# Moving gate steps between the halves of a head, loading W_qr by whole rows, and fetching the second group's tokens earlier in a four-block transformer kernel

## The chip, the cores and the metric

The kernel runs on one core of one Trainium2 chip. The metric is the device time of one execution in microseconds (us); the time of a version is the median of its runs. The engines are named as in the profile: PE is TensorE's matmul, PEld its weight load, DVE is VectorE, ACT is ScalarE, POOL is GpSimd, and SP is SyncE, which issues most plain DMAs here. POOL issues the indirect ones (gathers and scatters by row numbers).

## The reference

Everything is fp32; there are 16 sequences of 256 tokens, 512 wide, so 4096 tokens. Four blocks follow each other, each with a residual, the first three on a layer norm:

```python
x = x + conv_mix(layernorm(x), k, bias, ctx, ctx, 8)         # block 1
x = x + routed_and_shared_ffn(layernorm(x), gate_w, ...)     # block 2
x = x + latent_attention(layernorm(x), ctx, itok, W_...)     # block 3
x = x + gelu(x @ proj1.T + b1) @ proj2.T + b2                # block 4
```

- Block 1: within each channel group, all 8 x 8 products of heads of `v` and `x2` are convolved causally along the width of 512 with a filter per group (in the reference by FFT), `bias` times the product is added, and the result is summed with `x1`.
- Block 2: `logits = x @ gate_w` over 8 experts; the two largest are taken, their softmax are the gates. The result is the sum over the two chosen experts of gate times `gelu(x @ w1 + b1) @ w2 + b2` (hidden width 256), plus a shared FFN of width 512.
- Block 3: keys and values come from the context through a latent of 128, queries through a latent of 192; 16 heads of 128, and a rotary part of 64 in query and key (`W_qr`, `W_kr`). A query with segment number s sees the keys s-8 to s. The output goes through `W_o`.
- Block 4: a dense FFN of width 2048 with gelu.

## The kernel before

The work goes in tiles of 128 tokens and in stages, one after another on PE.

**Convolution, gates and shared FFN** (`conv_shared`, until about 980 us). One tile is a "head" h, 0 to 31. The causal convolution is done as matmuls with Toeplitz blocks: `conv` (L292) makes `y` from `kv` and `ut`, where `kv` holds the products of heads. Each head goes through `conv` in two halves of four column blocks `lc`. After each block, DVE multiplies and reduces `y` (`pr` L297, `oT` L304) and makes one block of the next half's `kv` (L274). Between the halves PE transposes the next head's inputs: `turn_inputs` makes `pvt` (L258), which needs the buffer that the last `kv` has read. The order of PE, DVE and ACT is the order of the program text here (`manual_schedule`); POOL and SP are placed by a scheduler by priorities. Small pieces of other work are given to `conv` as lists by `lc`: `one` for the first half, `two` for the second; lists `mid` and `end` are run between and after the halves.

The gates belong to groups of four heads, one group behind. With q = h % 4: q = 0 makes the logits, q = 1 runs `tops` in three steps, q = 2 makes row numbers (`slots`) and gate shares, and from q = 2 on rows of tokens are scattered to the experts (`send`, POOL L371). The steps of `tops`: step one finds the first maximum, step two the second, step three (L437 to L445) makes `ex` (difference, then an exponential on ACT), `both` (sum of the two one-hot rows) and four running counts `came`. In the kernel before all three stand in the first half, at `lc` 0, 1 and 2. `rank_rows`, at the end of the head, reads `both` and `came` on PE. The last tiles' gates are made in one piece each at the end of the stage.

**Routed experts** (`routed`, about 980 to 1300 us). 71 tiles of gathered rows (`xg`, four buffers), for each the two expert layers (L895, L914). Beside it, `beside` prepares the attention in steps numbered by the tile i: `head_weights` folds weight matrices through four rotating buffers `pre` (also to be had as `spare`), tile 12 loads the latent weights and `W_qr` (`load_latents(apart=True)`), tile 16 the routes (`load_routes`, which begins with an iota on POOL and works out `slot_s`, the rows of expert results of each sorted token), and from tile 20 on one step of the list `early` is run per tile: four `fetch` and three `fetch_keys`.

**Attention** (`attention_sorted`, about 1300 to 2243 us). Tokens are sorted by segment; T = 0 to 31 are tiles of sorted tokens, four to a group. For a tile, `fetch` gathers token rows and rotary rows (POOL L1902), `fetch_routed` the two rows of expert results, through four shared buffers `g_yt`, `fetch_keys` four windows of keys. `tokens` adds the expert results times their gates to the rows (DVE L1440), normalizes (`xh`, L72 and the statistics before it) and transposes on PE (`pt` L99; the rotary rows `prr` L1448). `latents` makes a group's `q1` and `q0` (`pq`, L1459), `heads` the queries of all heads (PE `pqr`, `pqn` L1487 to L1498), turned by the rotary angles on ACT, DVE and POOL (L1503 to L1507). Then per tile: `scores` (L1555), `weigh` (DVE transpose L1565, mask L1567, maximum), `weights` (exponential on ACT L1576, sum, division, transpose), `window` of the next tile (keys, ACT `kn` L1523, mask on DVE), `values`, and two tiles later `project` (`po`, L1611). Group 0 has its heads in two halves: after T = 0 and after T = 1, half of the pairs for the tiles 2 and 3. The second group's fetches (T = 4 to 7) come after T = 1 and T = 2 in the program, and its tokens after T = 2 and at T = 3. `issue_after(x)` keeps what is in it behind the instruction x in the scheduler's order. Outside `conv_shared` each engine's order is the scheduler's.

**Last FFN** (from about 2243 us): matmuls L1804 and L1862. No line of it is touched.

Of the kernel before, what the change touches and what calls it, by code (L numbers as in the profile page):

```python
# [42 lines left out]
class Kernel:  # L43
# [59 lines left out]
    def conv_shared(self, x1d, xgd):  # L103
        nc, tc, a = self.nc, self.tc, self.a
        with ExitStack() as ctx:
# [304 lines left out]
            def tops(r):  # L410
# [25 lines left out]
                def three():  # L436
                    r["ex"] = ex = g2("ex")  # L437
                    nc.vector.tensor_tensor(ex, r["m2"], r["m1"], ALU.subtract)
                    nc.scalar.activation(ex, ex, AF.Exp)
                    r["both"] = both = rp.tile([P, T4, E], F32, tag="both", name="both")[:, 0:n, :]  # L440
                    nc.vector.tensor_tensor(both, r["oh1"], r["oh2"], ALU.add)
                    for t in range(r["h"], r["h"] + n):
                        nc.vector.tensor_tensor(
                            came[:, t + 1, :], came[:, t, :], both[:, t - r["h"], :], ALU.add
                        )  # L445
# [297 lines left out]
            with tc.manual_schedule(engines=order):  # L743
                for h in range(HC):
# [19 lines left out]
                    if before is not None:  # L764
# [6 lines left out]
                        elif q == 1:  # L771
                            steps = tops(st["r"])
                            one = {k: [steps[k]] for k in range(3)}
# [185 lines left out]
    def load_latents(self, apart=False):  # L959
# [6 lines left out]
        if apart:  # L966
            f = R // 2
            for d in range(2):
                for c in range(2):
                    lo, to = (2 * d + c) * f, (2 * c + d) * f  # L970
                    nc.sync.dma_start(
                        self.wqr0.rearrange("q (h m) -> q h m", m=P)[:, :, to : to + f],
                        a["W_qr"][0:P, :].rearrange("q (h m) -> q h m", m=P)[:, :, lo : lo + f],
                    )
                    for i in range(2):
                        nc.sync.dma_start(
                            self.wqr1[i * (QC - P) : (i + 1) * (QC - P), :, to : to + f],
                            a["W_qr"][P:QC, :].rearrange("q (c i m) -> q c i m", i=2, m=P)[:, :, i, lo : lo + f],
                        )
            return  # L980
        nc.sync.dma_start(self.wqr0, a["W_qr"][0:P, :])
        for i in range(2):
# [3 lines left out]
            )  # L986

    def load_routes(self, tmp):
# [7 lines left out]
        nc.gpsimd.iota(  # L996
            start, pattern=[[ROOM, E]], base=0, channel_multiplier=0, allow_small_or_imprecise_dtypes=True
        )
# [62 lines left out]
    def beside(self, i, half, heads, early):  # L1061
# [4 lines left out]
        if half == 0:  # L1066
            heads(min(max(i - 2, 0), 2 * HEADS - 6))
            if i == 12:
                self.load_latents(apart=True)
            if i == 16:  # L1070
                self.load_routes(self.spare())
            if 20 <= i < 20 + len(early):
                early[i - 20]()
# [278 lines left out]
    def fetches(self, pool, x1d):  # L1352
# [7 lines left out]
        def fetch(T):  # L1360
            xs[T] = xt = tp.tile([P, D], F32, tag="xt", name="xt", bufs=XT_BUFS)
            self.fetch_rows(xt, x1f, self.order[:, T : T + 1], TOK)
            rrs[T] = rr = tp.tile([P, 2, P], F32, tag="rr", name="rr", bufs=4)
# [7 lines left out]
        return fetch, fetch_keys, xs, rrs, gws  # L1371

    def attention_sorted(self, fetched, ygd, x3s, end_of_queries):
        nc, tc = self.nc, self.tc
        wdq, m0, m1, wqr0, wqr1, nw = self.wdq, self.m0, self.m1, self.wqr0, self.wqr1, self.nw
        fetch, fetch_keys, xs, rrs, gws = fetched
# [5 lines left out]
        with ExitStack() as ctx:  # L1382
# [257 lines left out]
            for T in range(NT_ + 2):  # L1640
                g, t = T // T4, T % T4
                if T < NT_:
# [6 lines left out]
                    if nxt is not None:  # L1649
                        for k in () if g == 0 else ((0,), (2,), (), ())[t]:  # L1650
                            fetch((g + 1) * T4 + k)
                            fetch_routed(nxt, k)
                    if nxt is not None and g == 0 and t == 3:
# [6 lines left out]
                if T < NT_:  # L1660
# [3 lines left out]
                    if T < 2:  # L1664
                        for two in range(T * HP // 4, (T + 1) * HP // 4):
                            turned = heads(state[0], two, parts[1])
                    if nxt is not None and t == 3:
# [16 lines left out]
                if T < NT_ and nxt is not None:  # L1684
                    if g == 0:
                        if t == 1:
                            with tc.issue_after(turned):
                                for k in range(TH):
                                    fetch(T4 + k)
                                    fetch_routed(nxt, k)  # L1690
                        if t == 2:
                            for k in range(TH):
                                tokens(nxt, k)
                                fetch(T4 + TH + k)
                                fetch_routed(nxt, TH + k)
# [211 lines left out]
    def run(self, out):  # L1907
# [34 lines left out]
        with ExitStack() as experts:  # L1942
# [4 lines left out]
            with ExitStack() as stack:  # L1947
# [3 lines left out]
                early += [lambda t=t: fetched[1](t) for t in range(3)]  # L1951
                self.routed(xgd, ygd, early)
# [116 lines left out]
```

## Time and profile before

| what | value |
|---|---|
| median of 3 runs | 3085.8 us (3085.61 to 3088.05) |
| profiled execution, its own time | 3089.02 us |
| its span | 3087.2 us |
| PE busy | 3006.9 us (97%) |
| DVE busy | 1440.7 us (47%) |
| POOL busy | 912.5 us (30%) |
| ACT busy | 658.0 us (21%) |
| mean granted clock of PE | 0.99 of full speed |
| PE idle in wait of `kv` (L274) | 24.1 us, 11 times |
| PE idle in wait of `xh` (L72) | 24.4 us, 10 times |

A row of the timeline has start and duration in us, engine, line, operation, output and inputs, shape, how many instructions are drawn together (x4), and in brackets the idle time of the engine before it with what ended it. In a table by windows each row is a stretch of time: its length, the busy time of each engine with the number of instructions, the granted PE clock, the DMA engines' share and GB/s. Busy time that overlaps in other engines costs nothing; the span is set by what ends last, here PE almost throughout.

### The profile page before, as it was taken

What the parts mean: (1) busy time and instruction counts of PE and PEld (TensorE: products, weight loads), DVE (VectorE), ACT (ScalarE), POOL (GpSimd) and SP (SyncE); (2) the same over time, 40 slices, a digit from 0 to 9 for tenths busy, and PEclk for the clock granted to TensorE, in tenths of its full rate; (3) what the DMA queues carried; (4) which work ended last, traced back from release to release, by engine and by line L of the source; (5) the groups of instructions that cost most, each with busy time, mean ns of one, the idle gap of its engine ahead of it and who ended that gap; (6) DMA issues with size and microseconds to landing.
All of it is one profiled execution on the core that took longest, in us unless ns stands there. A gap on an engine that the chain in (4) does not pass through costs nothing.

```text
span 3087.2 us, 34716 instructions
## 1 busy us (share of the span) xinstructions
PE 3006.9 (97%) x12825; PEld 1530.4 (50%) x12825; DVE 1440.7 (47%) x2684; ACT 658.0 (21%) x1248; POOL 912.5 (30%) x1232
## 2 busy tenths in 40 slices
PE   8999999999999999898999999999999999999998
PEld 4444444544445666563554554554444444444443
DVE  6777777677674444443433433433433232222222
ACT  1111111111111121153333333323111111111110
POOL 2233332232234000066545545544110300301201
PEclk9999999999999999998999999999999999999999
DMA  4222211211216643312211211211221100100100
GB/s 118 69 99 85 69 57 53 75 53 55 65 44 192 183 155 128 110 53 64 90 49 49 82 56 50 74 49 58 73 102 28 55 14 14 55 11 8 47 1 29
DMA packets 124722, 209.87 MB, mean 68 GB/s; under 512 B 33864, under 2 KB 53736, under 8 KB 123904
## 3 DMA queue, kind: packets, MB, share of 16 engines
q1 hardware_dynamic: 96256, 125.63, 13.7%
q0 software_dynamic: 28288, 81.92, 8.3%
q8 instruction: 105, 1.72, 0.2%
q14 instruction: 73, 0.60, 0.1%
HBM read 140.12 MB, written 67.37 MB: 67 GB/s over the span
## 4 chain that ended last, share of the span: by engine, by line
PE 84%; DVE 6%; issue 5%; POOL 3%; DMA 1%; ACT 0%; SPq 0%; POOLq 0%; DVEq 0%; ACTq 0%
PE y L292 15%; PE po L1862 14%; PE ph L1804 12%; PE po L1611 8%; PE phg L895 4%; PE pog L914 4%; PE pout L503 4%; PE pqn L1490 4%; PE ph L490 3%; PE pqr L1487 2%; PE pqn L1498 2%; PE pt L99 2%; DVE oT L304 1%; PE pqr L1494 1%; DVE pr L297 1%
## 5 line engine op out<-in xcount | busy, mean ns | idle before, releaser
L292 PE MATMUL y<-kv,ut 128*128 128x512 f32 x1280 | 566.4, 598 | 0.6 <-DVE pr L297 0.6
L1611 PE MATMUL po<-nw,w 128*128 128x512 f32 x1024 | 445.7, 593 | 0.0
L1862 PE MATMUL po<-p,ht 128*128 128x512 f32 x1024 | 445.1, 592 | 0.0
L292 PEld LDWEIGHTS y<-kv,ut 128*128 128x128 f32 x1280 | 243.8, 193 | 298.8 <-issue 288.6
L1611 PEld LDWEIGHTS po<-nw,w 128*128 128x128 f32 x1024 | 192.0, 190 | 235.1 <-issue 229.6
L1862 PEld LDWEIGHTS po<-p,ht 128*128 128x128 f32 x1024 | 192.7, 190 | 233.4 <-issue 232.2
L1804 PE MATMUL ph<-w,w 128*128 128x512 f32 x640 | 281.2, 592 | 0.0
L297 DVE TENSOR_TENSOR pr<-y,cT 128x512 f32<-128x512 f32 x256 | 174.7, 682 | 149.5 <-PE y L292 149.3
L1866 DVE TENSOR_TENSOR res<-res,po 128x512 f32<-128x512 f32 x128 | 87.7, 685 | 314.7 <-PE po L1862 314.7
L1804 PEld LDWEIGHTS ph<-w,w 128*128 128x128 f32 x640 | 121.5, 190 | 152.6 <-issue 152.6
L304 DVE TENSOR_REDUCE oT<-pr 128x64 f32<-128x512 f32 x256 | 175.7, 686 | 8.8
L274 DVE TENSOR_TENSOR kv<-pvt,cT 128x512 f32<-128x512 f32 x256 | 174.1, 681 | 0.0
L1902 POOL DMA_INDIRECT gw<-kvd,keys_of x128 | 133.3, 1041 | 49.6 <-issue 37.3
L267 POOL TENSOR_TENSOR xt<-xt,sk 128x512 f32<-128x512 f32 x32 | 40.7, 1272 | 350.1 <-DVE sk L266 308.6
L1505 DVE TENSOR_TENSOR w<-pqr,w 128x512 f32<-128x512 f32 (+1 forms) x72 | 45.5, 632 | 201.9 <-ACT sw L1503 189.1
L895 PE MATMUL phg<-w,xTg 128*128 x568 | 134.6, 380 | 1.3 <-issue 0.7
L914 PE MATMUL pog<-w,hT 128*128 x284 | 133.6, 593 | 0.0
L490 PE MATMUL ph<-xT,w_s 128*128 128x512 f32 x256 | 117.2, 602 | 0.0
L1490 PE MATMUL pqn<-w,m 128*128 128x512 f32 (+1 forms) x288 | 116.5, 546 | 0.2 <-ACT kn L1523 0.2
L1804 PE MATMUL ph<-xT,w 128*128 128x512 f32 x256 | 116.4, 592 | 0.0
L503 PE MATMUL pout<-w_s,ht 128*128 128x512 f32 x256 | 115.3, 600 | 0.0
L1818 ACT ACTIVATE ht<-ht,p1b 128x512 f32<-128x512 f32 x96 | 69.3, 722 | 212.9 <-DVE ht L1823 212.9
(290 smaller groups left out, 3767.8 us busy)
## 6 DMA issues: line engine op xcount, KB each, us to landing
xg<-xgd SPq DMA_DIRECT2D x71, 256.0 KB, 2.8
ygd<-y SPq DMA_DIRECT2D x71, 256.0 KB, 2.0
xt<-in_x_dram SPq DMA_DIRECT2D x32, 256.0 KB, 4.7
ct<-in_ctx_dram SPq DMA_DIRECT2D x32, 256.0 KB, 3.4
ut<-in_kt_dram SPq DMA_DIRECT2D x32, 256.0 KB, 2.8
w<-in_w_dram SPq DMA_DIRECT2D x8, 1024.0 KB, 5.5
x1d<-xt SPq DMA_DIRECT2D x32, 256.0 KB, 2.8
x3s<-xt POOLq DMA_DIRECT2D x32, 256.0 KB, 2.7
```

Source lines behind the costliest of these rows:

```text
L274: nc.vector.tensor_tensor(c["kv"][half][:, mc, :].rearrange("p (b j i) -> p b j i", i=NH, j=NH), c["vt"][:, mc, cols].rearrange("p (b i) - ...
L292: c["conv"] = nc.tensor.matmul(y, ut[:, (lc - mc) * P : (lc - mc + 1) * P], kv[:, mc, :], start=(mc == 0), stop=(mc == lc),).ins
L297: nc.vector.tensor_tensor(pr, y.rearrange("p (b j i) -> p b j i", i=NH, j=NH), cT[:, lc, cols].rearrange("p (b i) -> p b i", i=NH) .unsque ...
L304: nc.vector.tensor_reduce(c["oT"][:, lc, cols].rearrange("p (b j) -> p b j", j=NH), pr, AX.X, ALU.add)
L490: nc.tensor.matmul(ph, w["sw1"][:, c, f * P : (f + 1) * P], xT[:, c, :], start=(c == 0), stop=(c == DC - 1),)
L503: nc.tensor.matmul(po, st["ht"][f][:, tok], w["sw2"][:, f, :], start=(f == 0), stop=(f == NC_ - 1))
L895: nc.tensor.matmul(ph, xT[:, c, :], w1[:, c, bass.ds(e * EH, EH)], start=(c == 0), stop=(c == DC - 1))
L914: nc.tensor.matmul(po, hT[:, q, :], w2[:, bass.ds(e * (EH * D // P) + q * D, D)], start=(q == 0), stop=(q == EH // P - 1),)
L1490: nc.tensor.matmul(pqn[k][i], m0[:, 2 * hp + i, :], q0, start=True, stop=False)
L1611: nc.tensor.matmul(po, ut[:, n].rearrange("p a j q -> p (a j q)"), nw[:, 2 * hp + i, :], start=(n == 0), stop=(n == HEADS - 1),)
L1804: nc.tensor.matmul(ph, w[:, c, :], x[:, c, :], start=(start and c == 0), stop=(c == half - 1), skip_group_check=True,)
L1862: nc.tensor.matmul(po, ht[f, i // T4][:, toks], w2[:, f, :], start=(f == fs[0]), stop=(f == fs[-1]))
```

## The change

- **Gate steps.** In `tops`, the four `came` sums go from DVE to POOL. At q = 1 step one stays at `lc` 0 of the first half, step two goes to `lc` 2, step three to `lc` 1 of the second half.
- **W_qr.** `load_latents(apart=True)` no longer loads `W_qr` by twelve strided DMAs. `load_turned`, called at tiles 12, 13 and 14, loads whole rows into a spare `pre` buffer and reorders them by two copies on POOL each time.
- **Early fetches.** The list `early` is kept behind the iota of `load_routes`, and gets four more steps that gather the token rows of T = 4 to 7 (`fetch_x`).
- **Second group.** After T = 0's and T = 1's rotations, the rotary and expert rows of T = 4 and T = 5 are fetched. At T = 2, right after the scores, `tokens` of T = 4 is issued (behind the last rotation), with the fetches of T = 6; later in T = 2 `tokens` of T = 5 and the fetches of T = 7. The old places after T = 1 and T = 2 are gone.

```diff
--- before.py
+++ after.py
@@ -440,7 +440,7 @@
                     r["both"] = both = rp.tile([P, T4, E], F32, tag="both", name="both")[:, 0:n, :]
                     nc.vector.tensor_tensor(both, r["oh1"], r["oh2"], ALU.add)
                     for t in range(r["h"], r["h"] + n):
-                        nc.vector.tensor_tensor(
+                        nc.gpsimd.tensor_tensor(
                             came[:, t + 1, :], came[:, t, :], both[:, t - r["h"], :], ALU.add
                         )
 
@@ -770,7 +770,7 @@
                             end.append(lambda: st.update(r=whole(st)))
                         elif q == 1:
                             steps = tops(st["r"])
-                            one = {k: [steps[k]] for k in range(3)}
+                            one, two = {0: [steps[0]], 2: [steps[1]]}, {1: [steps[2]]}
                             mid.append(lambda: hidden(st, 0))
                             end += [lambda: rank_rows(st["r"]), lambda: hidden(st, 1)]
                         elif q == 2:
@@ -964,19 +964,6 @@
             self.wdq[:, :, QC : 2 * P], a["W_dq"].rearrange("(c p) q -> p c q", p=P)[:, :, P:QC]
         )
         if apart:
-            f = R // 2
-            for d in range(2):
-                for c in range(2):
-                    lo, to = (2 * d + c) * f, (2 * c + d) * f
-                    nc.sync.dma_start(
-                        self.wqr0.rearrange("q (h m) -> q h m", m=P)[:, :, to : to + f],
-                        a["W_qr"][0:P, :].rearrange("q (h m) -> q h m", m=P)[:, :, lo : lo + f],
-                    )
-                    for i in range(2):
-                        nc.sync.dma_start(
-                            self.wqr1[i * (QC - P) : (i + 1) * (QC - P), :, to : to + f],
-                            a["W_qr"][P:QC, :].rearrange("q (c i m) -> q c i m", i=2, m=P)[:, :, i, lo : lo + f],
-                        )
             return
@@ -985,6 +972,26 @@
                 a["W_qr"][P:QC, :].rearrange("q (c i m) -> q c i m", i=2, m=P)[:, :, i, :],
             )
 
+    def load_turned(self, k, tmp):
+
+
+        nc, a = self.nc, self.a
+        n = 4 * P
+        if k < 2:
+            nc.sync.dma_start(tmp[:, 0:n], a["W_qr"][0:P, k * n : (k + 1) * n])
+            to = self.wqr0[:, k * n : (k + 1) * n].rearrange("q (h m) -> q h m", m=P)
+        else:
+            for i in range(2):
+                nc.sync.dma_start(
+                    tmp[i * (QC - P) : (i + 1) * (QC - P), 0:n].rearrange("q (c m) -> q c m", m=P),
+                    a["W_qr"][P:QC, :].rearrange("q (c i m) -> q c i m", i=2, m=P)[:, :, i, :],
+                )
+            to = self.wqr1
+        of = tmp[:, 0:n].rearrange("q (h d c f) -> q h d c f", d=2, c=2, f=R // 2)
+        to = to.rearrange("q h (c d f) -> q h c d f", c=2, d=2)
+        for c in range(2):
+            nc.gpsimd.tensor_copy(to[:, :, c, :, :], of[:, :, :, c, :])
+
     def load_routes(self, tmp):
 
         nc = self.nc
@@ -993,9 +1000,9 @@
         n = TOK // P
         slots = self.routes[:, :, 0:2].rearrange("p t k -> p k t")
         start = tmp[:, 2 * n * E : 2 * n * E + E]
-        nc.gpsimd.iota(
+        self.turned = nc.gpsimd.iota(
             start, pattern=[[ROOM, E]], base=0, channel_multiplier=0, allow_small_or_imprecise_dtypes=True
-        )
+        ).ins
         sums = tmp[:, 2 * n * E + E : 2 * n * E + E + 2 * n].rearrange("p (k t) -> p k t", k=2)
         cmp = tmp[:, 0 : 2 * n * E].rearrange("p (x e) -> p x e", e=E)
         flat = lambda t: t.rearrange("p k t -> p (k t)")
@@ -1067,10 +1074,13 @@
             heads(min(max(i - 2, 0), 2 * HEADS - 6))
             if i == 12:
                 self.load_latents(apart=True)
+            if 12 <= i < 15:
+                self.load_turned(i - 12, self.spare())
             if i == 16:
                 self.load_routes(self.spare())
             if 20 <= i < 20 + len(early):
-                early[i - 20]()
+                with self.tc.issue_after(self.turned):
+                    early[i - 20]()
 
 
     def attention(self, x1d, ygd, x3d):
@@ -1357,9 +1367,13 @@
         kvf = self.kvd.rearrange("b s c -> (b s) c")
         xs, rrs, gws = {}, {}, {}
 
-        def fetch(T):
+        def fetch_x(T):
             xs[T] = xt = tp.tile([P, D], F32, tag="xt", name="xt", bufs=XT_BUFS)
             self.fetch_rows(xt, x1f, self.order[:, T : T + 1], TOK)
+
+        def fetch(T):
+            if T not in xs:
+                fetch_x(T)
             rrs[T] = rr = tp.tile([P, 2, P], F32, tag="rr", name="rr", bufs=4)
             self.fetch_rows(rr.rearrange("p i f -> p (i f)"), self.roped, self.place[:, T : T + 1], S)
 
@@ -1368,12 +1382,12 @@
             for a in range(4):
                 self.fetch_rows(gw[:, a, :], kvf, self.keys_of[:, 4 * T + a : 4 * T + a + 1], TOK)
 
-        return fetch, fetch_keys, xs, rrs, gws
+        return fetch, fetch_keys, xs, rrs, gws, fetch_x
 
     def attention_sorted(self, fetched, ygd, x3s, end_of_queries):
         nc, tc = self.nc, self.tc
         wdq, m0, m1, wqr0, wqr1, nw = self.wdq, self.m0, self.m1, self.wqr0, self.wqr1, self.nw
-        fetch, fetch_keys, xs, rrs, gws = fetched
+        fetch, fetch_keys, xs, rrs, gws, _ = fetched
         T4 = 4
         N = T4 * P
         HP = HEADS // 2
@@ -1650,6 +1664,11 @@
                         for k in () if g == 0 else ((0,), (2,), (), ())[t]:
                             fetch((g + 1) * T4 + k)
                             fetch_routed(nxt, k)
+                    if nxt is not None and g == 0 and t == 2:
+                        with tc.issue_after(turned):
+                            tokens(nxt, 0)
+                        fetch(T4 + 2)
+                        fetch_routed(nxt, 2)
                     if nxt is not None and g == 0 and t == 3:
                         for k in range(TH, T4):
                             tokens(nxt, k)
@@ -1664,6 +1683,10 @@
                     if T < 2:
                         for two in range(T * HP // 4, (T + 1) * HP // 4):
                             turned = heads(state[0], two, parts[1])
+
+                        with tc.issue_after(turned):
+                            fetch(T4 + T)
+                            fetch_routed(nxt, T)
                     if nxt is not None and t == 3:
                         for two in range(HP // 2):
                             heads(nxt, two)
@@ -1683,16 +1706,10 @@
                         self.transposed(xT[:, :, k * P : (k + 1) * P], xh, ps_m, "m")
                 if T < NT_ and nxt is not None:
                     if g == 0:
-                        if t == 1:
-                            with tc.issue_after(turned):
-                                for k in range(TH):
-                                    fetch(T4 + k)
-                                    fetch_routed(nxt, k)
                         if t == 2:
-                            for k in range(TH):
-                                tokens(nxt, k)
-                                fetch(T4 + TH + k)
-                                fetch_routed(nxt, TH + k)
+                            tokens(nxt, 1)
+                            fetch(T4 + 3)
+                            fetch_routed(nxt, 3)
                     else:
                         if t == 0:
                             fetch((g + 1) * T4 + 1)
@@ -1949,6 +1966,7 @@
                 fetched = self.fetches(opened(stack), x1d)
                 early = [lambda t=t: fetched[0](t) for t in range(4)]
                 early += [lambda t=t: fetched[1](t) for t in range(3)]
+                early += [lambda t=t: fetched[5](t) for t in range(4, 8)]
                 self.routed(xgd, ygd, early)
                 ex = opened(experts)("e_x", 1, side="right")
                 self.e_w3 = ex.tile([P, 3 * DC // 2 * FF // 2], F32, name="w_3")
```

## The prediction

> **What bounds the kernel now.** I read the engines' busy shares first, then TensorE's waits, then the timelines around the waits the diff can touch.
>
> ```profile
> PE 3006.9 (97%) x12825; PEld 1530.4 (50%) x12825; DVE 1440.7 (47%) x2684; ACT 658.0 (21%) x1248; POOL 912.5 (30%) x1232
> ...
> PE pt L99 <- DVE xh L72: 24.4, 10, 8.2
> PE pvt L258 <- DVE kv L274: 24.1, 11, 3.6
> ```
>
> TensorE (PE) is busy for 3006.9 of 3087.2 us. Only its 80 us of idle time, and the time in which it works at half clock, can be won. Two groups hold most of the idle time, and the change touches both. The columns of the wait rows are us in all, times, longest.
>
> First group: in seven heads (h = 5, 9 ... 29) PE waits for `kv` between the two halves, 2.88 us in four of them and 1.22 to 1.23 us in three, 15.2 us together. VectorE's (DVE's) timeline at h = 13, then PE's:
>
> ```profile
> 392.77 0.68 DVE L274 TENSOR_TENSOR kv<-pvt,cT 128x512 f32<-128x512 f32 x1
> 393.37 0.15 DVE L438 TENSOR_TENSOR ex<-m,m 128x4 f32<-128x4 f32 x1
> 393.44 0.18 DVE L441 TENSOR_TENSOR both<-oh,oh 128x32 f32<-128x32 f32 x1
> 393.66 0.77 DVE L443 TENSOR_TENSOR came<-came,both 128x8 f32<-128x8 f32 x4
> 394.35 0.68 DVE L297 TENSOR_TENSOR pr<-y,cT 128x512 f32<-128x512 f32 x1
> ...
> 395.67 0.68 DVE L274 TENSOR_TENSOR kv<-pvt,cT 128x512 f32<-128x512 f32 x1
> 399.25 0.69 DVE L297 TENSOR_TENSOR pr<-y,cT 128x512 f32<-128x512 f32 x1 [2.90 <-PE y L292]
> ```
>
> ```profile
> 396.40 0.66 PE L258 MATMUL pvt<-ident,vh 128*128 128x128 f32 x4 [2.88 <-DVE kv L274]
> ```
>
> DVE works without a gap up to 396.3 and is what PE waits for; in the next half it idles 2.90 us, waiting for PE. Work taken out of the first half shortens the stall one for one; the second half takes it for nothing.
>
> Second group: the start of the attention, where 20 indirect gathers on GpSimd (POOL) start at 1371.72, one per 1.3 us, and the next tiles' tokens wait for them.
>
> ```profile
> 1371.72 1.04 POOL L1902 DMA_INDIRECT xt<-x1d,order  x1
> ...
> 1374.37 1.00 POOL L1902 DMA_INDIRECT w<-ygd,slot_s  x1 [0.30 <-issue]
> ```
>
> ```profile
> 1392.28 0.63 PE L99 MATMUL pt<-ident,xh 128*128 128x128 f32 x4 [2.82 <-DVE xh L72]
> ...
> 1401.08 1.09 PE L99 MATMUL pt<-ident,xh 128*128 128x128 f32 x4 [7.96 <-DVE xh L72]
> ...
> 1408.25 1.01 PE L99 MATMUL pt<-ident,xh 128*128 128x128 f32 x4 [1.50 <-DVE xh L72]
> ```
>
> With 0.68 us before `pq` that is 13.0 us idle. In two-us windows PE's granted clock is 0.50 from about 1395 to 1405 and again from 1409 to 1415; work in it costs about 4 us (`pq` takes 3.68 us instead of 2.0, T3's scores 3.3 instead of 1.8).
>
> **The change, part by part.** *1. Gate steps (L438 to L443, `two`).* Step three leaves the first half. `ex`, `both` and the four `came` hold DVE from the end of `kv` (393.37) to the start of `pr` (394.35): 0.98 us. The stalls become 1.90 and 0.25 us, 7 x 0.98 = **-6.9 us**. In the second half `ex` and `both` (0.33 us) go into the 2.90 us of idle; without that cover they would cost 7 x 0.33 = 2.3 us. The four `came` go to POOL, which is free there behind L267 (about 1.1 us at POOL's 0.19 to 0.29 for small operations); their reader, the ranking on PE, comes some 4 us later: nothing. ScalarE's exponential now stands between two gelus of the second half, with two more table loads in all; its `row` is read 9 us later: nothing.
>
> *2. The clock behind these stalls.* The one-us windows at h = 17, columns span, PE, PEld, DVE, ACT, POOL, granted clock, DMA share, GB/s:
>
> ```profile
> 514.00:515.00 1.00, 1.00 (x8) 1.00 (x7) 0.00 (x0) 0.00 (x0) 0.00 (x0) 0.56 0.00 0
> 515.00:516.00 1.00, 1.00 (x4) 0.48 (x3) 0.00 (x0) 0.59 (x1) 0.00 (x0) 0.50 0.00 0
> 516.00:517.00 1.00, 1.00 (x3) 0.48 (x2) 0.00 (x0) 0.00 (x0) 0.00 (x0) 0.50 0.00 0
> 517.00:518.00 1.00, 1.00 (x3) 0.38 (x2) 0.00 (x0) 0.00 (x0) 0.00 (x0) 0.74 0.00 0
> ```
>
> The stall of 2.88 us ended at 513.7, and 1.7 us is lost after it (0.44 + 0.50 + 0.50 + 0.26). The same follows at h = 5 and 9, not at 13: 5.1 us in all. The Trainium skill ("TensorE: Matmul & The Clock Gate", Part 1 and "HAM oscillation") says that gaps over about 3.4 us bring half speed. By that rule a stall of 2.88 us costs nothing beyond itself and this item is 0; the rows show it dropping the clock three times in four. Whether 1.90 us still does is not in the trace for this place: an idle of 2.01 us before 947.97 was followed by clock 0.50 at 952, 1.79 us before 129.92 by none. The 1.22 us stalls have none. Ends 0 and -5.1; 1.90 lies between the two nearest rows, so half: **-2.5 us**. By the rule alone the forecast below would stand 2.5 higher.
>
> *3. The last `came`.* At the end of the convolution POOL sends six tiles before it:
>
> ```profile
> 953.06 0.17 DVE L443 TENSOR_TENSOR came<-came,both 128x8 f32<-128x8 f32 x1
> ```
>
> ```profile
> 954.11 0.97 POOL L371 DMA_INDIRECT xgd<-xh,slots  x1 [0.30 <-issue]
> ```
>
> ```profile
> 954.71 0.37 PE L454 MATMUL prank<-came,ones 128*128 128x8 f32 x2
> ```
>
> It is ready at about 955.3, 0.6 after PE wants it: **+0.65 us** (0 to 1.1).
>
> *4. W_qr by whole rows.* Twelve issues on SP with 128-byte runs go; four whole-row loads into spare buffers come, with six POOL copies at about 0.73 us each (POOL's row for 128x256, L1507). DMA share is 0.99 and 1.00 from 980 to 1020, so this traffic is felt by the queues; but PE is 20.00 of 20.00 us busy from 1000 to 1020, and its only idle nearby is 1.25 us at 981 to 985. On SP, each next expert's rows load stands behind a W_qr load, which waits for a buffer; expert rows are asked for some 11 us ahead of their use, and the waits are about 1.5 us each. The early gathers now wait for the iota of the routes and land 60 us later, with 200 us to spare; so do the four added row gathers. **0** (-1.25 to +3).
>
> *5. Start of the attention.* I walked each engine's new order with the old durations. POOL is now to issue, between T0's and T1's rotations, the rotary row of T4, its two gate gathers, then T6's two (which share buffers with T4's and so wait for DVE to have read those), T3's keys, T8's two, and only then T1's rotations. DVE has T4's two gated sums between the transpose and the mask of T1's scores. Behind the gather of T4's row stand, in order on DVE: mask, maximum, softmax; behind these ScalarE's exponential and `kn`; behind that PE's queries.
>
> ```profile
> 1357.17 0.72 DVE L1565 STREAM_TRANSPOSE e<-ps 128x512 f32<-128x512 f32 x1 [0.76 <-PE ps L1555]
> 1357.92 0.96 DVE L1567 TENSOR_TENSOR e<-e,mask 128x512 f32<-128x512 f32 x1
> ```
>
> POOL finishes T0's rotations at 1358.3 and issues T4's first gate gather at 1359.7. The gather before took from 1374.37 to its reader at 1377.89, 3.5 us: DVE goes on at 1363.3 instead of 1357.9, and with the second sum 7.0 us late. `kn` comes at 1368.0 instead of 1360.97, PE loses **+7.0 us**; DVE's rotations behind it add **+1.7**. T2's scores come 9 us later, T1's rotations standing behind T8's gathers on POOL; the values' matmuls of T0 (13.9 us) start 14.6 us later, since PE also waits **+4.6** for the first transposed tokens of T4 (1386.9). That is 13.3 us idle against 13.0. In return T5 to T7 are ready when PE reaches them: none of the three old waits, and `pq` starts at 1409.0 (1409.94 before) at full clock. `pq` then ends 3.5 us earlier than 1418.0. Each of the two new gaps can drop the clock as above (1.7 us each): -3.5 + 3.4 is about 0, without the penalties -3.5; I take **-1** (-6 to +5).
>
> *Sum:* -6.9 - 2.5 + 0.65 + 0 - 1 = -9.8 us. The profiled execution took 3089.0 us, 1.8 over its span of 3087.2; it would take 3079.3. It lies 3.2 above the median of the runs, 3085.8; by the same difference the median becomes **3076.0 us**. 0.2%, or 6.2 us, is about what a measurement of this kernel can tell from no change: below 3079.6 is faster, over 3092.0 slower.
>
> **The rivals.** *a) The attention's new waits stay.* The +7.0 and +1.7 hold, the added 4.6 is made good and nothing else comes back: -6.9 - 2.5 + 0.65 + 8.7 = 0, 3085.8. For it: POOL is 16.4 of 20 us busy from 1380 to 1400. Against it: the old waits of 13.0 us were on POOL's chain, which now starts 12 us earlier.
>
> *b) Slower: DVE's in-order wait on T4's gathers decides.* All 13.3 us are lost, the clock drops after both (3.4 us), and none of the 13.0 is returned, because T5 to T7 wait on POOL as before. +16.7 - 8.75 = +7.9: **3093.7**. It takes over 15 us lost in the attention to reach 3092.
>
> *c) Gate and attention both pay.* No clock drop after 1.90 us, and the old waits vanish with DVE less late: -6.9 - 5.1 + 0.65 - 6 = -17.4, 3068.4.
>
> *d) The step does not do what it says.* DVE refills the freed 0.98 us, or PE then waits as long for ScalarE's `vh`: only +0.65 - 1 remain, 3085.5. Against it: DVE's row is gapless up to the stall.
>
> **How the numbers follow.** The likeliest, 0.55: 3076.0, its own range 3069 to 3082 from the clock (0 to -5.1) and the attention (-6 to +5). a 0.15, b 0.11, c 0.11, d 0.08. Faster: c and 0.9 of the first, 0.61. Slower: b and a little of a's upper end, 0.14. Same: the rest, 0.25. The range 3067 to 3088 leaves out b, the upper end of a and the low end of c, about 0.2.
>
> **What would show it.** In the profile after: seven stalls at L258 of 1.90 and 0.25 us, with no L438 to L443 on DVE ahead of them, and `came` on POOL; clock 1.00 in the windows behind; a wait of `prank` under 1 us; no new wait of L895; at the attention, DVE waiting for `w` before the mask of T1, a wait of L1490 for `kn` of about 7 us, one of L99 of 4.6 us and none after. Wrong would be: stalls unchanged at L258, L1490 waiting over 10 us, or expert matmuls waiting for weights.

## The result: 3075.0 us, 11.4 us less

The changed kernel takes 3074.96 us (median of six runs, 3074.05 to 3075.8) against 3086.32 us of the kernel before, run beside it (3085.61 to 3088.64). The ratio is 0.9962, 95% interval 0.9949 to 0.9975. The forecast was 3076.0 (3067 to 3088): 9.8 us less than 3085.8. Its own profiled execution has a span of 3073.5 us, 13.7 below the other profile; the profile of before was 2.7 us above its median, this one 0.3.

First the page's busy line, then TensorE's waits (us in all, times, longest), of the changed kernel:

```profile
PE 3000.4 (98%) x12825; PEld 1529.7 (50%) x12825; DVE 1434.6 (47%) x2652; ACT 661.8 (22%) x1250; POOL 921.1 (30%) x1270
...
PE pvt L258 <- DVE kv L274: 17.3, 11, 3.6
PE pt L99 <- DVE xh L72: 15.5, 7, 8.3
PE pqn L1504 <- ACT kn L1537: 7.1, 1, 7.1
```

The wait for `kv` fell by 6.8 us. The wait for `xh` fell by 8.9 us, and a new one stands in its place: queries (L1504) waiting 7.1 us for keys. 32 instructions left VectorE, all of them running counts, and went to GpSimd.

VectorE's timeline in the changed kernel at h = 13, both halves, then TensorE's:

```profile
386.00 0.68 DVE L297 TENSOR_TENSOR pr<-y,cT 128x512 f32<-128x512 f32 x1
386.72 0.69 DVE L304 TENSOR_REDUCE oT<-pr 128x64 f32<-128x512 f32 x1
387.33 0.68 DVE L274 TENSOR_TENSOR kv<-pvt,cT 128x512 f32<-128x512 f32 x1
390.91 0.69 DVE L297 TENSOR_TENSOR pr<-y,cT 128x512 f32<-128x512 f32 x1 [2.90 <-PE y L292]
...
395.35 0.15 DVE L438 TENSOR_TENSOR ex<-m,m 128x4 f32<-128x4 f32 x1
395.42 0.18 DVE L441 TENSOR_TENSOR both<-oh,oh 128x32 f32<-128x32 f32 x1
395.52 0.69 DVE L297 TENSOR_TENSOR pr<-y,cT 128x512 f32<-128x512 f32 x1
```

```profile
388.06 0.65 PE L258 MATMUL pvt<-ident,vh 128*128 128x128 f32 x4 [1.91 <-DVE kv L274]
```

`ex` and `both` now stand in the second half, after VectorE's own 2.90 us of idle time, and no running count follows them. TensorE's stall went from 2.88 to 1.91 us; the other six went the same way, to 1.9 or 0.25.

At the attention's start, VectorE's timeline and TensorE's waits:

```profile
1345.00 0.72 DVE L1579 STREAM_TRANSPOSE e<-ps 128x512 f32<-128x512 f32 x1 [0.75 <-PE ps L1569]
1351.20 0.75 DVE L1454 SCALAR_TENSOR_TENSOR xt<-w,routes,xt 128x512 f32<-128x512 f32 x1 [5.48 <-DMA w<-ygd,slot_s]
1351.87 0.69 DVE L1581 TENSOR_TENSOR e<-e,mask 128x512 f32<-128x512 f32 x1
```

```profile
1356.36 1.22 PE L1504 MATMUL pqn<-w,m 128*128 128x256 f32 x2 [7.14 <-ACT kn L1537]
...
1367.70 0.42 PE L1563 MATMUL ps<-w,kn 128*32 128x128 f32 x8 [1.67 <-ACT w L1525]
...
1375.53 0.70 PE L99 MATMUL pt<-ident,xh 128*128 128x128 f32 x4 [3.36 <-DVE xh L72]
```

VectorE stands 5.48 us at T4's gathered row, with T1's mask and softmax behind it, and TensorE loses 7.14 us two engines later. In the kernel before, the same queries hardly waited:

```profile
1361.59 0.70 PE L1490 MATMUL pqn<-w,m 128*128 128x256 f32 x2 [0.20 <-ACT kn L1523]
```

Later in the changed kernel TensorE waits 3.36 us for T4's tokens. The three old waits (2.82, 7.96, 1.50) are gone.

Where the 13.7 us between the two profiles lie, by the same instructions in both:

| stretch | before, us | changed, us | difference |
|---|---|---|---|
| start to the stall of h = 5 (code not touched) | 155.5 | 153.5 | -2.0 |
| from there to the end of the stall of h = 29 | 708.5 | 698.3 | -10.2 |
| to the first expert matmul | 117.7 | 118.0 | +0.4 |
| to the attention's first `prr` | 319.3 | 318.7 | -0.6 |
| to the output projection `po` of T1 | 151.5 | 149.8 | -1.7 |
| to the end | 1634.8 | 1635.2 | +0.4 |

The first row is no gain: nothing of the change runs there, and the experiments' traces have 151.8 to 156.5 us for the same code. The second row is 7 x 0.98 = 6.9 us of stall and, as the clock table below shows, two clock drops of 1.7 us. In a second trace of the changed kernel (the last experiment) the third to fifth rows are 117.7, 318.9 and 150.0 us, so the 0.4 is no more than traces of one kernel differ by. The old order of the attention has one trace with which to compare (151.5); the new one has four between 149.3 and 150.0 outside the first set below.

### The profile page after: what moved, and what is told of

Same layout as the page of the kernel before. It is cut to its first block, busy times and chain, and to the rows that moved or that the text cites. A ratio compares the mean times of both kernels' runs of the same rounds, so it can differ in the third digit from the quotient of the medians.

```text
span 3073.5 us, 34728 instructions
## 1 busy us (share of the span) xinstructions
PE 3000.4 (98%) x12825; PEld 1529.7 (50%) x12825; DVE 1434.6 (47%) x2652; ACT 661.8 (22%) x1250; POOL 921.1 (30%) x1270
## 4 chain that ended last, share of the span: by engine, by line
PE 87%; DVE 6%; issue 4%; POOL 2%; DMA 1%; ACT 0%; SPq 0%; POOLq 0%; DVEq 0%; ACTq 0%
PE y L292 15%; PE po L1879 14%; PE ph L1821 13%; PE po L1625 11%; PE phg L895 4%; PE pog L914 4%; PE pqn L1504 4%; PE pout L503 3%; PE ph L490 3%; PE pqr L1501 2%; PE pqn L1512 2%; PE pt L99 2%; PE pqr L1508 1%; DVE pr L297 1%; PE ptg L884 1%
## 5 line engine op out<-in xcount | busy, mean ns | idle before, releaser
L1504 PE MATMUL pqn<-w,m 128*128 128x512 f32 (+1 forms) x288 | 117.0, 548 | 7.2 <-ACT kn L1537 7.1
L490 PE MATMUL ph<-xT,w_s 128*128 128x512 f32 x256 | 118.4, 607 | 0.0
```

What stands on the lines that cost most here:

```text
L490: nc.tensor.matmul(ph, w["sw1"][:, c, f * P : (f + 1) * P], xT[:, c, :], start=(c == 0), stop=(c == DC - 1),)
L1504: nc.tensor.matmul(pqn[k][i], m0[:, 2 * hp + i, :], q0, start=True, stop=False)
```

## The experiments

Three sets of runs, each on one chip beside the kernel before. On the first set's chip the kernel before takes 3115.8 us, on the second's 3086.1 and on the third's 3084.6; comparisons go by the ratio to before on the same chip. By that ratio the changed kernel is at 0.9962.

**The parts by themselves.** The gate steps alone:

```diff
-                            one = {k: [steps[k]] for k in range(3)}
+                            one, two = {0: [steps[0]], 2: [steps[1]]}, {1: [steps[2]]}
...
-                        nc.vector.tensor_tensor(
+                        nc.gpsimd.tensor_tensor(
                             came[:, t + 1, :], came[:, t, :], both[:, t - r["h"], :], ALU.add
                         )
```

> Kernel before with the gate steps and the running counts alone moved (parts 1 to 3). Theory of the stalls: the seven stalls are 1.90 and 0.25 us, -6.9 us, and the clock after them gives 0 to -5.1 more; with 0.65 back at the end of the convolution the time falls by 6 to 11 us, to about 3077. Rival (the step does not do what it says, the gain of the changed kernel comes from the routed stage and the attention): within 2 us of before.

3106.82 us, ratio 0.9966 (0.9954 to 0.9978): nine tenths of the whole change's gain, 10.5 us of 3086. TensorE's stall at h = 13:

```profile
391.12 0.66 PE L258 MATMUL pvt<-ident,vh 128*128 128x128 f32 x4 [1.91 <-DVE kv L274]
```

The stalls are 1.90, 1.90, 1.91, 1.90, 0.25, 0.26 and 0.24 us. The theory of the stalls holds, and with it falls the rival that the step does nothing.

The attention's start alone (the early list with the added row fetches, and the moved fetches and tokens, without the gate steps and `W_qr`):

```diff
+                early += [lambda t=t: fetched[5](t) for t in range(4, 8)]
...
+                        with tc.issue_after(turned):
+                            fetch(T4 + T)
+                            fetch_routed(nxt, T)
```

> Kernel before with the early fetches and the new order at the start of the attention alone (part 5). Theory: two groups of waits of about 13 us change places, the late tokens come in time, the time is 1 to 3 us below before; the wait of the queries for the keys is 7 us. Rival (the new waits are made good by nothing): 5 to 9 us above before. Rival (all old waits vanish): 6 us or more below.

3119.52 us, ratio 1.0008 (1.0000 to 1.0017): no gain on this chip, rather 2.5 us lost, at the edge of the interval. None of the three forecasts of the time came true, though the new wait for the keys is there:

```profile
1392.28 1.22 PE L1495 MATMUL pqn<-w,m 128*128 128x256 f32 x2 [7.11 <-ACT kn L1528]
```

From `prr` to `po` of T1 this kernel takes 153.5 us, and the two kernels of this set with the old order take 153.4 and 153.8, so the attention itself is even. What is lost is in the routed stage: 341.6 us from the first expert matmul to `prr`, against 335.4 and 337.2 (see the last section). This part was run alone on this chip only.

`W_qr` alone:

```diff
+            if 12 <= i < 15:
+                self.load_turned(i - 12, self.spare())
```

> Kernel before with W_qr by whole rows alone (part 4). Theory: TensorE is busy throughout the stage, so within 1.3 us of before, on either side. Rival (the strided loads had held back the experts' rows): over 3 us below; rival (the loads that wait for buffers hold back SP): over 3 us above, with waits of the expert matmuls for weights.

3115.32 us, ratio 0.9997 (0.9989 to 1.0005). Nothing that can be measured, as expected; of the rivals, three us to either side, the slower is outside the interval and the faster at its edge.

The running counts back on VectorE, in the second half:

```diff
-                        nc.gpsimd.tensor_tensor(
+                        nc.vector.tensor_tensor(
                             came[:, t + 1, :], came[:, t, :], both[:, t - r["h"], :], ALU.add
                         )
```

> Changed kernel with the four running counts back on VectorE, in the second half. Theory: VectorE idles 2.9 us there, so the seven stalls stay 1.90 and 0.25 us and the time is that of the changed kernel within 1 us (the end of the convolution 0 to 0.65 us shorter). Rival (GpSimd's part is what counts): the stalls come back by 0.77 us each, 5 us above the changed kernel.

3107.56 us, ratio 0.9965 (0.9951 to 0.9979), against 0.9962; the stalls are 1.90 and 0.25 us again. The engine that makes the counts does not matter: the half in which they are made does. Beside the gate steps alone (0.9966 on the same chip) this kernel has `W_qr`, the early list and the attention's part as well, and it is no faster here, where the moved list costs about 4 us in the routed stage (last section). So of the change's parts only the gate steps are shown to gain.

**How far the second half goes.** Step two moved as well:

```diff
-                            one, two = {0: [steps[0]], 2: [steps[1]]}, {1: [steps[2]]}
+                            one, two = {0: [steps[0]]}, {1: [steps[1]], 2: [steps[2]]}
```

> Changed kernel with step two moved to the second half as well (column blocks 1 and 2 there for steps two and three). Step two holds VectorE 1.22 us. Theory: the stalls become 0.68 us four times and vanish three times, 4 x 1.22 + 3 x 0.25 = 5.6 us less, and the last clock drop behind h = 17 goes too (1.7 us): 5 to 7.5 us below the changed kernel. Rival (the second half has no more room: the ranking on TensorE waits for both and the counts): the ranking waits 0.5 us or more seven times, and 2 us or less are won.

3066.04 us, ratio 0.9933 (0.9919 to 0.9946), 9 us below the changed kernel by the ratios. TensorE's timeline at h = 13:

```profile
387.29 0.66 PE L258 MATMUL pvt<-ident,vh 128*128 128x128 f32 x4 [0.68 <-DVE kv L274]
```

The stall is 0.68 us, as 1.90 - 1.22 says; the last three are gone, the ranking does not wait, and no clock drop follows. 5.6 of stall and 1.7 of clock are 7.3 of the 9; the rest is less than the interval's width.

All three steps moved:

```diff
-                            one, two = {0: [steps[0]]}, {1: [steps[1]], 2: [steps[2]]}
+                            two = {0: [steps[0]], 1: [steps[1]], 2: [steps[2]]}
```

> Changed kernel with all three steps in the second half (column blocks 0, 1, 2). Theory of the room: VectorE's idle time there is 2.90 + 1.11 us and the steps take 2.8; the seven stalls vanish, 8.4 us less, unless the ranking becomes the wait: then it waits about 1 us in each group and the time is equal to or above the one with only steps two and three there.

3074.5 us, ratio 0.9965 (0.9951 to 0.9978): all of the gain of moving step two is lost. TensorE's timeline at h = 13:

```profile
387.14 1.12 PE L262 MATMUL psk<-z,ones_b 128*128 128x512 f32 x2 [0.68 <-ACT cT L100]
...
399.12 0.41 PE L454 MATMUL prank<-came,ones 128*128 128x32 f32 x2 [0.44 <-POOL came L443]
```

The stall for `kv` is gone in all seven heads, and two waits take its place: 0.68 us for the transposed context, which ScalarE copies behind a gelu, and 0.44 us for the counts. No clock drop follows either. The expectation had the ranking's wait in it, not ScalarE's. From stall to stall four heads take 116.16 us; with two steps moved 115.13 and in the changed kernel 116.34. The two listed waits are 1.12 us against 0.68, so some 0.6 of the 1.03 us lies in gaps too small for the rows, and was not followed.

**The order at the attention's start.** VectorE's tokens of T4 behind T1's softmax, and T6's fetches on GpSimd behind T1's rotations:

```diff
-                        with tc.issue_after(turned):
+                        with tc.issue_after(turned), tc.issue_after(last_at[0]):
                             tokens(nxt, 0)
-                        fetch(T4 + 2)
-                        fetch_routed(nxt, 2)
+                        with tc.issue_after(turned):
+                            fetch(T4 + 2)
+                            fetch_routed(nxt, 2)
```

> Changed kernel with the tokens of T4 kept on VectorE behind the softmax of T1, and the fetches of T6 on GpSimd behind T1's rotations. Theory of the in-order waits: the wait of 7.1 us for the keys goes, T2's scores come some 6 us earlier, T5 to T7 stay in time, and 8 to 13 us are won over the changed kernel, about 3064. Rival (gathers on GpSimd are the bound whatever the order): the wait moves to the transposes of T4 and T5 and 3 us or less are won.

3068.85 us, ratio 0.9941 (0.9928 to 0.9955): 6.5 us below the changed kernel by the ratios, between theory (8 to 13) and rival (3 or less). `prr` to `po` of T1 takes 144.2 us, 5.6 less than in the changed kernel and 7.3 less than before. TensorE's waits there, then GpSimd's rows before them:

```profile
1362.86 0.43 PE L1563 MATMUL ps<-w,kn 128*32 128x128 f32 x8 [3.00 <-ACT w L1525]
1364.49 0.43 PE L1569 MATMUL ps<-w,krz 128*32 128x64 f32 x16 [1.20 <-POOL w L1521]
...
1371.01 1.09 PE L99 MATMUL pt<-ident,xh 128*128 128x128 f32 x4 [3.69 <-DVE xh L72]
```

```profile
1353.56 1.00 POOL L1920 DMA_INDIRECT gw<-kvd,keys_of  x1 [0.30 <-issue]
...
1358.72 1.42 POOL L1520 TENSOR_TENSOR sw<-sw,w 128x256 f32<-128x256 f32 x2
...
1368.24 0.21 POOL L70 TENSOR_TENSOR ln_rs<-ln_mv,eps 128x1 f32<-128x1 f32 x1
1368.60 1.02 POOL L1920 DMA_INDIRECT rr<-roped,place  x1 [0.15 <-issue]
1369.65 0.58 POOL L71 TENSOR_TENSOR ln_rs<-ln_rs,mhalf 128x1 f32<-128x1 f32 x1
```

The wait for the keys is gone (0.2 us). What is left goes back to GpSimd: T1's rotations stand behind T3's four key gathers (from 1353.56), and T4's normalization, split in two, among gathers of T5 and T6.

VectorE's order mended alone:

```diff
-                        with tc.issue_after(turned):
+                        with tc.issue_after(turned), tc.issue_after(last_at[0]):
                             tokens(nxt, 0)
```

> Changed kernel with only VectorE's order mended (tokens of T4 behind the softmax of T1), fetches of T6 left free to stand ahead of T1's rotations. If VectorE's head is what held the queries, the wait for the keys goes here as well; what the run with both has over this one is GpSimd's share, 0 to 5 us by its gathers ahead of the rotations (1.3 us each).

3074.26 us, ratio 0.9962 (0.9948 to 0.9975): nothing over the changed kernel. What the run with both mends has over it is 5.4 us by the medians, just over the 0 to 5 that were expected for GpSimd's share. TensorE's timeline:

```profile
1349.77 0.70 PE L1504 MATMUL pqn<-w,m 128*128 128x256 f32 x2 [0.21 <-ACT kn L1537]
...
1361.03 0.66 PE L1563 MATMUL ps<-w,kn 128*32 128x128 f32 x8 [3.71 <-ACT w L1525]
1368.15 0.65 PE L1569 MATMUL ps<-w,krz 128*32 128x64 f32 x16 [6.46 <-POOL w L1521]
```

The 7.1 us for the keys do go, so VectorE's in-order wait did cause them. They come back at T2's scores, as 3.7 and 6.5 us for the turned queries, whose rotations stand on GpSimd among gathers of expert rows for later tiles:

```profile
1357.18 1.04 POOL L1919 DMA_INDIRECT w<-ygd,slot_s  x1 [0.16 <-issue]
...
1364.33 1.00 POOL L1919 DMA_INDIRECT w<-ygd,slot_s  x1 [1.15 <-DVE xt L1454]
1365.35 1.41 POOL L1520 TENSOR_TENSOR sw<-sw,w 128x256 f32<-128x256 f32 x2
```

Two queues were late by nearly the same time, and mending VectorE's shows only GpSimd's. GpSimd's order mended alone was not run.

**Together.** Step two in the second half and both mends of the order:

```diff
-                            one, two = {0: [steps[0]], 2: [steps[1]]}, {1: [steps[2]]}
+                            one, two = {0: [steps[0]]}, {1: [steps[1]], 2: [steps[2]]}
...
-                        with tc.issue_after(turned):
+                        with tc.issue_after(turned), tc.issue_after(last_at[0]):
                             tokens(nxt, 0)
-                        fetch(T4 + 2)
-                        fetch_routed(nxt, 2)
+                        with tc.issue_after(turned):
+                            fetch(T4 + 2)
+                            fetch_routed(nxt, 2)
```

> Changed kernel with step two in the second half and with both mends of the attention's order. The two places are independent, so the gains add: about 9 us from the steps (5.6 of stall, the rest the clock) and 6 from the order, near 15 us below the changed kernel. Rival (the gains overlap or the clock takes them back): 10 us or less.

3059.85 us, ratio 0.9913 (0.9898 to 0.9928): 14.2 us below the changed kernel on the same chip, nearly the sum of the two (9 and 6.5). It is the fastest version of this study, 24.8 us below the kernel before by the medians.

With T3's key gathers behind T1's rotations and T4's normalization ahead of T5's gathers as well (all of this diff), and with the normalization alone (its last two lines):

```diff
-                    if 3 <= T + 2 < NT_:
+                    if 4 <= T + 2 < NT_:
                         fetch_keys(T + 2)
...
                         with tc.issue_after(turned):
+                            if T == 1:
+                                fetch_keys(3)
                             fetch(T4 + T)
...
-                        with tc.issue_after(turned), tc.issue_after(last_at[0]):
+                        with tc.issue_after(last_at[0]):
                             tokens(nxt, 0)
```

> As e9, and on GpSimd T3's four key gathers stand behind T1's rotations and T4's normalization ahead of the gathers of T5. In the run with the order mended TensorE still waits 4.2 us for the queries' rotations of T2's scores and 3.7 us for T4's normalized rows, both behind gathers on GpSimd. Theory (position on GpSimd alone): both go, 6 to 8 us below e9. Rival (T3's keys become late): a wait of the key transposes of 2 us or more, and 3 us or less won.

> As e9, and only T4's normalization on GpSimd stands ahead of the gathers of T5; T3's key gathers stay ahead of T1's rotations. Theory: the 3.7 us for T4's rows go, the 4.2 us for the rotations stay, so about 3 to 4 us below e9 and as much above the run with both.

3063.3 us (0.9927, 0.9913 to 0.9940) and 3061.61 us (0.9920, 0.9907 to 0.9934): not below the run without them. The theory is missed in both; of the first, the rival (T3's keys become late) came true. TensorE's timeline with both edits, then the same `pq` in the run without them:

```profile
1348.39 0.43 PE L1563 MATMUL ps<-w,kn 128*32 128x128 f32 x8 [1.10 <-ACT w L1525]
...
1355.42 0.47 PE L1535 MATMUL pkw<-ident,gw 128*128 128x128 f32 x1 [1.29 <-DMA gw<-kvd,keys_of]
...
1357.83 15.87 PE L1625 MATMUL po<-nw,w 128*128 128x512 f32 x32
...
1375.23 0.63 PE L99 MATMUL pt<-ident,xh 128*128 128x128 f32 x4 [1.32 <-DVE xh L72]
...
1381.78 0.70 PE L99 MATMUL pt<-ident,xh 128*128 128x128 f32 x4 [2.46 <-DVE xh L72]
1383.16 3.68 PE L1473 MATMUL pq<-w,w_dq 128*64 128x512 f32 x8 [0.68 <-ACT w L100]
```

```profile
1383.27 1.94 PE L1473 MATMUL pq<-w,w_dq 128*64 128x512 f32 x8 [0.67 <-ACT w L100]
```

The waits aimed at shrink (the turned queries 3.13 to 1.10, T4's rows 3.48 to 1.32), and `po` of T0 starts at 1357.83, 79.4 us after `prr` instead of 83.7. But T3's keys are late by 2.8 us in three pieces, and the last tokens come when they came before: T7's is a wait again, and after it `pq1` takes 3.68 us, where it takes 1.94 in the run without these edits. With the second edit alone T7's rows are late too, by 3.04 us. From `prr` to `po` of T1: 144.1 us without, 147.5 with both, 146.2 with the second. Here an order of GpSimd's gathers that served one tile starved another.

The changed kernel once more, on the third chip:

> The changed kernel itself once more, beside the mended ones on the same chip: 0.9962 of before, as first measured, if the chip has no long waits in the routed stage.

3074.09 us, ratio 0.9959 (0.9945 to 0.9973): the same as at first.

**The clock behind the stalls.** In every trace, the granted clock over the 8 us after each wait for `kv`, which is 0.79 where it drops and 1.00 where not. First the seven heads that the change touches:

| stall, us | kernels | stalls | clock 0.79 |
|---|---|---|---|
| 2.88 | before, the attention alone, `W_qr` alone | 12 | 10 |
| 1.90 | changed (two traces), gates alone, counts on VectorE, the two with only the attention's order mended | 24 | 6, one in each trace |
| 1.23 and less | all but the one with all three steps late, which has none | 43 | 0 |

Then four stalls at the start of the stage, before h = 5, whose code is the same in all fourteen traces:

| stall, us | stalls | clock dropped |
|---|---|---|
| 1.67 and 1.88 | 28 | 0 |
| 1.75 to 1.80 | 14 | 7 (0.79) |
| 3.59 | 14 | 14 (0.62 to 0.82) |

The length of a stall does not decide by itself: 1.88 us at one place never dropped the clock, and 1.78 us at another did in half of the traces, the changed kernel's among them, but not in that of the kernel before. The stall in the changed kernel, then the 8 us after it there and in the kernel before (1.79 us):

```profile
126.22 0.72 PE L258 MATMUL pvt<-ident,vh 128*128 128x128 f32 x4 [1.78 <-DVE kv L274]
```

```profile
126.22:134.22 8.00, 8.00 (x21) 4.28 (x22) 3.40 (x6) 0.59 (x1) 0.71 (x1) 0.79 0.01 2
```

```profile
129.92:137.92 8.00, 8.00 (x25) 4.17 (x26) 5.05 (x8) 0.59 (x1) 1.26 (x1) 1.00 0.14 33
```

Two windows behind touched stalls of before and two of the changed kernel (span, PE, PEld, DVE, ACT, POOL, granted clock, DMA share, GB/s):

```profile
396.40:404.40 8.00, 8.00 (x25) 4.17 (x26) 5.05 (x8) 0.59 (x1) 1.27 (x1) 1.00 0.11 32
513.72:521.72 8.00, 8.00 (x21) 4.34 (x22) 3.40 (x6) 0.59 (x1) 0.73 (x1) 0.79 0.00 0
```

```profile
388.06:396.06 8.00, 8.00 (x25) 4.16 (x26) 5.08 (x10) 2.07 (x3) 1.57 (x3) 1.00 0.12 33
504.40:512.40 8.00, 8.00 (x21) 3.99 (x22) 3.57 (x6) 1.87 (x2) 0.90 (x1) 0.79 0.00 0
```

A drop costs 0.21 x 8 = 1.7 us. Per execution 3.3 drops became 1: 2.3 x 1.7 = 4 us over all traces, 3.4 between the two profiles compared.

## Why the prediction was right

*Gate steps, -6.9.* Right to a tenth: 7 x 0.98 by the stalls of every run that has them. VectorE's row without a gap up to the stall was the proof, and the stalls shortened one for one.

*Clock, -2.5.* Right in kind, too small: 3.4 to 4. The half was a choice between two rows, 2.01 us with a drop and 1.79 without. The runs put 1.90 us at one drop in four, which leaves more gain than half. The Trainium skill ("TensorE: Matmul & The Clock Gate", "HAM oscillation") lets gaps up to about 3.4 us pass; stalls of 2.88 us dropped the clock ten times in twelve here, so the measurement decides. What the same page calls a free-running window (Part 1) would make such a drop a matter of chance by phase, as the rows of 1.90 and 1.78 us look; no run shows the window itself. That the half came out near was in part luck: the row of 1.79 us without a drop was one draw, and the same stall is followed by a drop in the changed kernel.

*Last running count, +0.65.* The cost was 0, because the forecast had the wrong reader. The gates alone show it:

```profile
946.19 0.37 PE L454 MATMUL prank<-came,ones 128*128 128x8 f32 x2
```

```profile
946.59 0.22 POOL L443 TENSOR_TENSOR came<-came,both 128x8 f32<-128x8 f32 x1
```

```profile
947.35 0.28 PE L522 MATMUL pcount<-came,ones 128*128 128x8 f32 x2
```

The ranking runs before the last count is begun: it reads the counts up to the tile before (`came[:, h : h + n, :]`). The reader of the last one is `pcount`, and TensorE now has a piece of the shared FFN (L490) between the two, so it does not idle. The stretch is 0.4 us longer in the one trace and 0.0 in the other.

*W_qr, 0.* Right: ratio 0.9997 alone. The stretch up to the attention is 0.6 us shorter, and traces of the changed routed stage alone differ by as much (318.7 to 319.3).

*Attention, -1.* Right in sum: -1.7 between the two profiles, 0 on the slower chip. Of its terms, +7.0 was 7.1 (6.9 over the 0.20 of before); +4.6 for T4's tokens was 3.4. The +1.7 was given to VectorE's rotations; TensorE waited there for ScalarE's copies (1.67) and GpSimd's rotations (0.89), where it had waited 0.34 and 0.68 before, so 1.5 more. The output projection `po` of T0 (the forecast's matmuls of 13.9 us) began 16.8 us later than before, counted from the attention's own start, where 14.6 was said. The waits were shorter than said, but TensorE's clock was low behind each of them: T2's scores took 0.67 us a piece instead of 0.40. By an estimate from the one-us windows from 1345 to 1382 (busy time times the clock that is missing) that costs about 6 us, where the walk put 3.4; behind the old waits the same sum is 5.0, where it put 4. The return came as said in kind: T5 to T7 in time and `pq1` 1.94 us instead of 3.68. But `pq` ended 1.7 us earlier, not 3.5. That a net of terms this large came within 0.7 us of the forecast is in part luck.

*Sum.* -6.9 - 3.4 + 0.4 - 0.6 - 1.7 = -12.2 by stretches that the change touches, against -11.4 by the medians and -9.8 forecast. The rival that comes nearest, without clock drops and with every old wait gone, gave -17.4; the one with new waits made good by nothing gave 0. The latter's mechanism (VectorE in order behind a gather) was there in full, and only what it freed later made it even.

## What to carry to other kernels

Small work on an engine that is not the bottleneck can be free in one half of a loop and cost one for one in the other, as here: look where that engine idles within the iteration, and move the work there until a second chain appears (here after the second step, not the third). When an early fetch is taken forward, look at what stands behind its reader and behind its issue on both engines; where two queues are equally late, as VectorE's and GpSimd's here, mending one can gain nothing. A stall's price includes the clock after it, 1.7 us a drop here: on top of their own microseconds, shorter stalls dropped it less often (ten in twelve at 2.88 us, one in four at 1.90, none at 1.23 and less), though no length between can be called safe by these traces.

## What was not expected

On the first set's chip every kernel has a stop in the routed stage that no other trace has, at the time of the early gathers: without the moved list at about 990 to 1014, with it at about 1060 to 1096. The same window in the profile of the kernel before (which is not from this set), then of the gates alone on this chip:

```profile
990.00:1010.00 20.00, 20.00 (x92) 13.83 (x91) 9.11 (x19) 2.50 (x8) 15.42 (x16) 1.00 1.10 305
```

```profile
990.00:1010.00 20.00, 6.50 (x22) 4.42 (x23) 3.50 (x9) 0.62 (x2) 11.80 (x12) 0.66 0.58 161
```

In it TensorE works 6.5 of 20 us, and the DMA engines move 161 GB/s instead of 305. TensorE's longest waits are there for an expert's transposed rows (`xTg`), and in part for nothing that the profile names (the gates alone, then the attention alone):

```profile
1003.82 3.47 PE L895 MATMUL phg<-w,xTg 128*128 x8 [11.14 <-DVE xTg L885]
```

```profile
1094.67 0.69 PE L906 MATMUL pth<-ident,hs 128*128 128x128 f32 x2 [8.56 <-issue]
```

The waits of the stop add up to 13.8 and 12.1 us in the two traces with the 20 gathers of the list before, and to 17.4 and 16.4 us in the two with the 24 of the changed list. That is where the attention alone lost on that chip. The stop moves when the list moves, so it goes with the early gathers; why they hold up the rest on this chip stays open, and no run took them apart. Some 8 us more by which this chip is slower lie after `po` of T1 and were not followed.
